# The last unit of a bidirectional state-space mixer gets an order of its own, with the first sequence's spectra and taps inside it

## The chip, the core and the metric

The kernel runs on one core of a Trainium2 chip. A core has TensorE (PE, matrix products; its weight loads are listed as PEld), VectorE (DVE), ScalarE (ACT), GpSimd (POOL) and SyncE (SP, which here issues the DMAs). Each engine works through its own queue in order and waits on semaphores for the others. Matrix products land in PSUM, everything else lies in SBUF; large arrays lie in HBM. The metric is the device time of one execution in microseconds.

## The reference

The input is x, 8 sequences of 1024 tokens with 128 channels, in float32. Layer 0 is a group norm and an attention with 4 heads. Layer 1 has two parts, each added to its input, each behind a layer norm over the channels:

```
t = t + h_f + h_b           # two selective state-space mixers on ln(t), forward and on the reversed sequence:
                            #   project to z, x, B, C, dt; causal convolution of 4 taps; silu;
                            #   chunks of 64: Y = (C B^T * decay) xdt + C state exp(A); state passes on
                            #   y = (Y + D x) * silu(z), scaled by rsqrt(mean y^2), times out_proj
t = t + stu(ln(t))          # spectral filters: out = sum_k  fftconv(phi_k, u) * sigma_k^0.25 * M_k
                            #   (for U+ and U-), plus taps: sum over i < 3 of shift(u, i) * M_u[i]
```

`stu` is taken from one of four banks, which a hard gumbel choice selects.

## The kernel before, in words

`fast_kernel` (L46) has four parts: attention; the mixer; the first spectral stage (forward transforms and taps); and the second (products per frequency, L1412 to L1490, and the transform back, L1514).

**The mixer** runs over 16 units, `Unit(b, d)`: sequence b, direction d = 0 or 1. All five queues follow the order in which the program text issues (`ALL_IN_ORDER`). One pass of the loop at L1194 does unit u, and beside it the tail of the unit before (`last`) and the beginning of the next (`following`). A unit's own steps are:

- `turn_x` (L946): x turned on PE (sx), times dt on DVE (xdt). `weigh_start` (L859): ec on POOL. `turn_b` (L964): B turned and C B^T (sb), copied by ACT (bg). `between` (L854): exp of the decays lm on ACT.
- `decayed_x` (L982): bg masked causally and xdd, on DVE. `project_z`, `activate_z` (L910, L915): pz on PE, silu on ACT (zs).
- `chunk_states` (L992): pst on PE. `pass_states` (L1009): one copy and 28 small DVE steps, each on the one before; after chunks 7 and 14 DMAs copy states to the other half of the partitions (moved).
- `weigh_decays` (L1036): lm times bg on DVE, in two halves. `outputs` (L1044): 64x64 matmuls into sy.
- The tail: `add_x` (L1074) y from sy on DVE; `gate` (L1089) y times zs on DVE, its square on ACT; `end` (L1165): `project_out` (spo), `square_sums` (misc) with a copy by ACT (sums), `turn_sums` (rms_v on DVE, rms on POOL); `scale_rows` (L1133) on ACT; `add_rows` (L1139) into the residual X[b] on DVE, and for d = 1 a store to xd; `reload` (L1145) brings X[b] back in another token order, four neighbouring tokens to a partition.

After the loop, L1285 to L1292 do the last unit's tail alone. PSUM is divided into two pools of two buffers each, `ps_w` and `ps_s`; a buffer is written again when its last reader is done.

**Layer norm** is split: `normalize` (L444) takes the statistics (8 bn_stats and 8 bn_aggr on DVE, `rsqrt` on POOL), `normalized` (L453) a shift on DVE and 8 activations on ACT (ln_x). In the loop, units with d = 1 normalize sequence b + 2 for the mixer; the last unit normalizes sequence 0 in its reloaded form, for the spectral stage.

**The first spectral stage** (L1388) is one loop over b, 0 to 8, with PE, DVE, ACT and POOL in order. `transform(b)` (L1328): 8 transposes of ln_x into cpt; two blocks of 4 products with the cosine and sine table (pf); a copy by ACT (later), two sums on DVE (sd), 6 sums on POOL (sp); a store to ud in HBM; and cpt copied by ACT into ut. `regress(b, k)` (L1369): 12 products of shifted ut with the taps (pu), added to X by DVE. `turned(n)` (L1311) turns a quarter of the mixing matrices (md, mdt, me) and shares cpt's PSUM buffer. One pass does the transform of b, normalizes b + 1, and does the taps of b - 1; then X[b - 1] is stored to xa.

Of the kernel before, what the change touches and what calls it, by code (L numbers as in the profile page):

```python
# [45 lines left out]
def fast_kernel(ctx: ExitStack, tc: tile.TileContext, a: dict, out: bass.AP, bad: bass.AP):  # L46
# [477 lines left out]


# [236 lines left out]
    with ExitStack() as s:  # L762
# [219 lines left out]
        def decayed_x(u):  # L982

            nc.vector.tensor_tensor(u.gm, u.gm, upto[u.d].unsqueeze(1).to_broadcast([P, NT, L]), ALU.mult)
            u.xdd = p1.tile([P, NT, NH, HP], F32, tag="xdd", name=f"xdd{u.tag}")
            for i in range(2):
                js = slice(4 * i, 4 * i + 4)
                nc.vector.tensor_tensor(
                    u.xdd[:, js], u.xdt[:, js], u.rest.rearrange("p h j -> p j h")[:, js].unsqueeze(3).to_broadcast([P, 4, NH, HP]), ALU.mult
                )  # L990
# [18 lines left out]
        def pass_states(u):  # L1009

            u.state = p1.tile([P, 2 * NT - 1, 2, HP], F32, tag="state", name=f"state{u.tag}")
            u.moved = p1.tile([P, NT, 2, HP], F32, tag="moved", name=f"moved{u.tag}")
            for k, (j, c) in enumerate(u.chunks[:-1]):
                if k == 0:
                    nc.vector.tensor_copy(u.state[:, 0], u.pst[c][:, j])
                else:
                    for h in range(2):
                        nc.vector.scalar_tensor_tensor(  # L1018
                            u.state[:, k, h, :],
                            u.state[:, k - 1, h, :],  # L1020
                            u.dec[:, c, h, j : j + 1],
                            u.pst[c][:, j, h, :],
                            ALU.mult,
                            ALU.add,
                        )
                if k in (7, 14):
                    for r in range(2):

                        ks = [m for m in range(0 if k == 7 else 8, k + 1) if u.chunks[m + 1][1] != r]
                        to = slice((1 - r) * L, (2 - r) * L)  # L1030
                        nc.sync.dma_start(
                            u.moved[to, ks[0] // 2 : ks[-1] // 2 + 1],
                            u.state[r * L : (r + 1) * L, ks[0] : ks[-1] + 1 : 2],
                        )
# [39 lines left out]
        def add_x(u):  # L1074

            u.y = p1.tile([P, 2, T], F32, tag="y", name=f"y{u.tag}")
            by_chunk = "p (j c l) -> p c j l"
            for n in range(2):
                for c in range(2):
                    nc.vector.scalar_tensor_tensor(  # L1080
                        u.y[:, n, :].rearrange(by_chunk, j=NT, c=2)[:, c],
                        u.xs[:, n, :].rearrange(by_chunk, j=NT, c=2)[:, c],
                        dcol[u.d][:, n : n + 1],
                        u.py[c][:, n],
                        ALU.mult,
                        ALU.add,
                    )
# [6 lines left out]
        def project_out(u, js):  # L1094
            if js[0] == 0:
                u.po = wide_psum(ps_s, f"spo{u.tag}").rearrange("p (j e) -> p j e", j=NT)
# [68 lines left out]
        def end(u):  # L1165

            project_out(u, range(4))
            misc = wide_psum(ps_s, f"misc{u.tag}")
# [25 lines left out]
        for at, u in enumerate(units):  # L1194
            following = units[at + 1] if at + 1 < len(units) else None
# [4 lines left out]
            if following and u.d == 1:  # L1200
                turn_decays(following)
            if at == 0:
                between(u, AF.Relu, 1.0)
            if following:
                take_decays(following)
# [8 lines left out]
            if following:  # L1214
                project_x(following, 0)
                copy_x(following, 0)
# [3 lines left out]
            if following:  # L1220
                project_x(following, 1)
                copy_x(following, 1)
            if early_decays:
                add_decays(after_it)
            decayed_x(u)
            weigh_decays(u, 0)
            if last:
                end(last)
            if early_decays:
                turn_decays(after_it)  # L1230
            if following:
                first_tap(following, 0)
            if last:
                scale_rows(last)
            b = u.b + 2 if following else 0
            norm = None
            if u.d == 1 and b < B:
# [6 lines left out]
            if following:  # L1244
                convolve(following, 0, range(pad - 1))
# [4 lines left out]
            if following:  # L1250
                first_tap(following, 1)
            if norm:
                mv = norm[0]
                norm = mv, rsqrt(bridge, mv[:, :, 1], NT, 1.0, 1e-5, "ln_r")
                if following:
                    behind(begun[-1], following.convolved, "beside the states")
            if following:
                from_row(following, following.convolved)
# [3 lines left out]
            norming = normalized(b, bridge, *norm) if norm else iter(())  # L1262
# [4 lines left out]
            if following:  # L1267
                convolve(following, 0, range(pad - 1, pad))
                activate_x(following, 0)
                between(following, AF.Relu, 1.0)  # L1270
                project_bc(following)
                activate_bc(following)
                convolve(following, 1)
# [3 lines left out]
            if following:  # L1277
                activate_x(following, 1)
# [5 lines left out]
            last = u  # L1284
        add_x(last)  # L1285
        for n in range(2):
            gate(last, n)
        end(last)
        scale_rows(last)
        add_rows(last)  # L1290
        reload(last)
# [7 lines left out]
    with ExitStack() as s:  # L1299
# [4 lines left out]
        with ExitStack() as s2:  # L1304
# [23 lines left out]
            def transform(b):  # L1328
# [3 lines left out]
                for j in range(NT):  # L1332
                    nc.tensor.transpose(pt[:, j // 4, j % 4, :], un[:, j // 4, j % 4, :], ident)  # L1333
                sp = p2.tile([P, NF // FC, NB, 2, 4, FC], F32, tag="sp", name=f"sp{b}")
                for k in range(NB):
                    pf = ps_f.tile([P, 4, 2, NF], F32, tag="f", name=f"pf{b}_{k}")
                    for r in range(4):
                        nc.tensor.matmul(  # L1338
                            pf[:, r].rearrange("p i f -> p (i f)"),
                            lhsT=un[:, k, r, :],  # L1340
                            rhs=fwd[:, r].rearrange("p i f -> p (i f)"),
                            start=True,
                            stop=True,
                        )

                    sd = p2.tile([P, 2, 2, 2, NF], F32, tag="sd", name=f"sd{b}_{k}")
                    later = p2.tile([P, 2, 2, NF], F32, tag="later", name=f"later{b}_{k}")
                    nc.scalar.copy(  # L1348
                        later.rearrange("p r i f -> p (r i f)"), pf[:, 2:4].rearrange("p r i f -> p (r i f)")
                    )  # L1350
                    for i, op in enumerate((ALU.add, ALU.subtract)):
                        nc.vector.tensor_tensor(sd[:, i], pf[:, 0:2], later, op)  # L1352
                    to = sp[:, :, NB - 1 - k].rearrange("p c i q f -> p q i c f")
                    sd = sd.rearrange("p s r i (c f) -> p s r i c f", f=FC)
                    for q, op in ((0, ALU.add), (2, ALU.subtract)):
                        nc.gpsimd.tensor_tensor(to[:, q], sd[:, 0, 0], sd[:, 0, 1], op)

                    for q, i, op in ((1, 0, ALU.add), (1, 1, ALU.subtract), (3, 0, ALU.subtract), (3, 1, ALU.add)):
                        nc.gpsimd.tensor_tensor(to[:, q, i], sd[:, 1, 0, i], sd[:, 1, 1, 1 - i], op)  # L1359
                nc.sync.dma_start(  # L1360
                    ud[:, :, b].rearrange("c p k i q f -> p c (k i q f)"), sp.rearrange("p c k i q f -> p c (k i q f)")
                )

                ut = uts[b] = p2.tile([P, 4, NB * P + 1], F32, tag="ut", name=f"ut{b}")
                nc.gpsimd.memset(ut[:, :, 0:1], 0.0)
                for k in range(NB):
                    nc.scalar.copy(ut[:, :, 1 + k * P : 1 + (k + 1) * P], pt[:, k])

            def regress(b, k):  # L1369

                xq = X[b].rearrange("p (k r) c -> p k r c", k=NB)
                po = ps_o.tile([P, 4, C], F32, tag="o", name=f"pu{b}_{k}")
                for r in range(4):
                    for i in range(KU):
                        at = 1 + k * P - (i > r)
                        nc.tensor.matmul(  # L1376
                            po[:, r, :],
                            lhsT=uts[b][:, (r - i) % 4, at : at + P],
                            rhs=m_u[:, i, :],
                            start=(i == 0),  # L1380
                            stop=(i == KU - 1),
                        )
                nc.vector.scalar_tensor_tensor(xq[:, k], po, keep[:, k : k + 1], xq[:, k], ALU.mult, ALU.add)
# [3 lines left out]
            norms[1] = normalize(p2, 1)  # L1387
            for b in range(B + 1):  # L1388
# [7 lines left out]
                if b:  # L1396
                    regress(b - 1, 0)
                    if b <= 4:
                        turned(b - 1)
                    regress(b - 1, 1)  # L1400
                    nc.sync.dma_start(xa[b - 1].rearrange("p k r c -> p (k r) c"), X[b - 1])
# [957 lines left out]
```

## Time and profile before

| | |
|---|---|
| time, median of 3 runs | 1477.29 us (1474.59 to 1480.68) |
| the profiled execution, its time | 1471.66 us |
| its span | 1469.9 us |
| mean granted clock of PE | 0.978 |
| PE busy | 1340.2 us (91%) |
| PEld busy | 841.3 us (57%) |
| DVE busy | 1095.4 us (75%) |
| ACT busy | 912.9 us (62%) |
| POOL busy | 505.9 us (34%) |
| HBM read, written | 78.15 MB, 34.08 MB |

Busy time is the time in which an engine has an instruction in work; matmuls are pipelined and their ends are modelled, so a busy PE is not one at its peak. The granted clock is the share of full speed that the throttle gave PE. In rows of the timeline the columns are start, length, engine, line, operation, output and inputs, count; in rows of waits: total, times, longest. Line numbers are those of the kernel before.

In the trace the last unit's own work begins with sx at 1009.49 us, its row scaling ends at 1058.2, and the first spectral stage's first transposes (cpt) begin at 1058.27. The first product of the second spectral stage (pg) begins at 1151.23.

### The profile page before, as it was taken

What the parts mean: (1) busy time and instruction counts of PE and PEld (TensorE: products, weight loads), DVE (VectorE), ACT (ScalarE), POOL (GpSimd) and SP (SyncE); (2) the same over time, 40 slices, a digit from 0 to 9 for tenths busy, and PEclk for the clock granted to TensorE, in tenths of its full rate; (3) what the DMA queues carried; (4) which work ended last, traced back from release to release, by engine and by line L of the source; (5) the groups of instructions that cost most, each with busy time, mean ns of one, the idle gap of its engine ahead of it and who ended that gap; (6) DMA issues with size and microseconds to landing.
All of it is one profiled execution on the core that took longest, in us unless ns stands there. A gap on an engine that the chain in (4) does not pass through costs nothing. (4 is left out here: it accounts for less than half of the span.)

```text
span 1469.9 us, 45286 instructions
## 1 busy us (share of the span) xinstructions
PE 1340.2 (91%) x19782; PEld 841.3 (57%) x19782; DVE 1095.4 (75%) x2138; ACT 912.9 (62%) x1421; POOL 505.9 (34%) x510
## 2 busy tenths in 40 slices
PE   5999999999998889998989899998599899999977
PEld 2323333333333556665656566655489899999963
DVE  6788888788767687878787877787555577777755
ACT  3766666766765777777777777666355455555520
POOL 3336966866201332323232323233186211111100
PEclk9999999999999999999999999999799999999989
DMA  7101111110002334444444444341258422322258
GB/s 182 35 1 30 44 36 37 51 50 9 8 1 58 74 73 98 92 91 96 90 95 90 92 91 97 88 90 29 69 191 218 128 76 68 91 71 76 68 144 322
DMA packets 139382, 123.09 MB, mean 84 GB/s; under 512 B 44808, under 2 KB 118152, under 8 KB 135080
## 3 DMA queue, kind: packets, MB, share of 16 engines
q1 hardware_dynamic: 137064, 115.93, 30.8%
q10 hardware_dynamic: 2112, 4.19, 0.7%
q8 instruction: 157, 2.57, 0.7%
q14 instruction: 49, 0.40, 0.1%
HBM read 78.15 MB, written 34.08 MB: 76 GB/s over the span
## 5 line engine op out<-in xcount | busy, mean ns | idle before, releaser
L633 ACT ACTIVATE pr<-pt 128x1024 f32<-128x1024 f32 x256 | 247.9, 1021 | 114.3 <-PE pt L628 112.7
L658 DVE TENSOR_TENSOR two<-pr,pr 128x1024 f32<-128x1024 f32 x128 | 162.8, 1312 | 20.7 <-ACT pr L633 19.8
L1433 ACT COPY gs<-pg 128x512 f32<-128x512 f32 x256 | 132.5, 602 | 63.4 <-PE pg L1420 47.5
L1431 DVE COPY gs<-pg 128x512 f32<-128x512 f32 x256 | 158.8, 684 | 14.1 <-PE pg L1420 8.9
L628 PE MATMUL pt<-q,k 32*128 32x512 f32 x1024 | 159.3, 653 | 7.0 <-ACT pr L633 4.7
L1420 PE MATMUL pg<-taps,mst 32*128 32x128 f32 x4096 | 145.2, 280 | 4.4 <-ACT gs L1433 3.5
L1420 PEld LDWEIGHTS pg<-taps,mst 32*128 32x128 f32 x4096 | 133.3, 188 | 16.4 <-issue 11.4
L649 PE MATMUL po<-pr,v 128*32 128x512 f32 x1024 | 139.3, 602 | 0.0
L925 PE MATMUL pb<-bxt,wbc 128*128 128x512 f32 x256 | 115.6, 604 | 14.7 <-ACT zs L916 14.7
L1454 PE MATMUL py<-gs,u 128*32 128x128 f32 (+1 forms) x4096 | 127.8, 277 | 0.2 <-DVE gs L1431 0.2
L861 POOL TENSOR_TENSOR ec<-ec,ct 128x2048 f32<-128x2048 f32 x16 | 72.6, 4536 | 153.1 <-ACT ct L941 141.0
L903 DVE SCALAR_TENSOR_TENSOR xs<-xp,cw,xs 128x1024 f32<-128x1024 f32 x96 | 121.8, 1282 | 4.6 <-issue 1.7
L1454 PEld LDWEIGHTS py<-gs,u 128*32 128x32 f32 (+1 forms) x4096 | 112.0, 140 | 7.5 <-DVE gs L1431 0.4
L1443 POOL TENSOR_SCALAR u<-u 128x512 f32<-128x512 f32 x16 | 24.0, 1497 | 227.2 <-DMA u<-ud 120.1
L628 PEld LDWEIGHTS pt<-q,k 32*128 32x128 f32 x1024 | 47.6, 186 | 85.5 <-issue 32.3
L1129 POOL TENSOR_TENSOR rms<-rms_v,mhalf 128x8 f32<-128x8 f32 x16 | 27.9, 1742 | 187.5 <-DVE rms_v L1127 187.5
L925 PEld LDWEIGHTS pb<-bxt,wbc 128*128 128x128 f32 x256 | 47.7, 191 | 73.1 <-issue 59.1
L1018 DVE SCALAR_TENSOR_TENSOR state<-state,dec,pst 128x64 f32<-128x64 f32 x448 | 87.3, 275 | 1.1
L848 POOL TENSOR_TENSOR lm<-cs,lm 128x2048 f32<-128x2048 f32 x16 | 57.9, 3621 | 60.6 <-DVE sp_u L508 30.8
L649 PEld LDWEIGHTS po<-pr,v 128*32 128x32 f32 x1024 | 27.7, 109 | 88.2 <-issue 84.1
L1099 PE MATMUL spo<-wo,y 128*128 128x128 f32 x512 | 71.0, 288 | 7.9 <-DVE y L1091 7.8
L957 DVE TENSOR_TENSOR xdt<-sx,dt 128x1024 f32<-128x1024 f32 x32 | 37.9, 1220 | 52.9 <-PE sx L954 52.9
(278 smaller groups left out, 2797.9 us busy)
## 6 DMA issues: line engine op xcount, KB each, us to landing
lm<-cd SPq DMA_DIRECT2D x32, 512.0 KB
ec<-cd SPq DMA_DIRECT2D x32, 512.0 KB
ud<-sp SPq DMA_DIRECT2D x8, 1024.0 KB
u<-ud SPq DMA_DIRECT2D x32, 256.0 KB
yd<-sums SPq DMA_DIRECT2D x32, 256.0 KB
moved<-state SPq DMA_DIRECT2D x48, 128.0 KB
yt<-yd SPq DMA_DIRECT2D x6, 1024.0 KB
X<-in_x SPq DMA_DIRECT2D x8, 512.0 KB
```

The costliest lines, as they stand in the source:

```text
L628: nc.tensor.matmul(pt[:, i, :], lhsT=k[rows, j * P : (j + 1) * P], rhs=q[rows, cols], start=True, stop=True)
L633: nc.scalar.activation(pr[:, 2 * g : 2 * g + 2, :].rearrange("p i t -> p (i t)"), pt.rearrange("p i t -> p (i t)"), AF.Exp, scale=SCALE,)
L649: nc.tensor.matmul(po[rows, :], lhsT=vs[b][:, j, rows], rhs=pr[:, h, :], start=(j == 0), stop=(j == NT - 1))
L658: nc.vector.tensor_tensor(two, sums["pr"][:, 2 * g : 2 * g + 2, :], pr[:, 2 * g : 2 * g + 2, :], ALU.add)
L861: t = nc.gpsimd.tensor_tensor(u.ec, u.ec, u.ct.unsqueeze(1).to_broadcast([P, NH, NT, L]), ALU.mult)
L903: u.convolved = nc.vector.scalar_tensor_tensor(acc, xp[:, at : at + T], cw[u.d][:, n, i : i + 1], acc, ALU.mult, ALU.add)
L925: nc.tensor.matmul(u.pb[:, i * 512 : (i + 1) * 512], lhsT=wbc[u.d][:, k, :], rhs=xt[:, at : at + 512], start=(k == 0), stop=(k == KC - 1),)
L1018: nc.vector.scalar_tensor_tensor(u.state[:, k, h, :], u.state[:, k - 1, h, :], u.dec[:, c, h, j : j + 1], u.pst[c][:, j, h, :], ALU.mult, ...
L1420: nc.tensor.matmul(pts[g][:, e, :], lhsT=mst[rows, n * 4 + e, :], rhs=taps[rows, cols].rearrange("p f q m i -> p (f q m i)"), start=True, ...
L1431: nc.vector.tensor_copy(to, frm)
L1433: nc.scalar.copy(to, frm)
L1454: nc.tensor.matmul(py[t * 32 : t * 32 + 32 - 16 * m, q // 2, :], lhsT=u[:, i, m:, :, :, q * FC + f].rearrange("p k b i -> p (k b i)"), rhs ...
```

## The change

The loop over units ends before the last one, and the last unit is written out by hand. In it, `decayed_x` comes before the masking (now `causal`), z is projected before the states, `pass_states` takes the chunks it shall do and is called twice, and `end` is given its PSUM pool. The bodies of `transform` and `regress` become functions of their own (same operations), and for sequence 0 they are called inside the last unit, with tiles that reuse buffers of the mixer (ut0, sp0, sd0). Sequence 0 is normalized in unit (6, 1); sequence 1's statistics are taken in unit (7, 0) and its activations are made in the last unit. The loop of the first spectral stage begins at b = 1. The operations of the whole kernel are the same in kind, shape and number.

```diff
-            b = u.b + 2 if following else 0
+            b = (u.b + 2) % B
             norm = None
-            if u.d == 1 and b < B:
+            if u.d == 1 or u.b == B - 1:
                 norm = normalize(bridge, b, later=True)
...
-            norming = normalized(b, bridge, *norm) if norm else iter(())
+            norming = normalized(b, bridge, *norm) if u.d else iter(())
...
+        u = units[-1]
+        un = xns.pop(0).rearrange("p (k r) c -> p k r c", k=NB)
+        turn_x(u)
+        weigh_start(u, u.convolved)
+        turn_b(u)
+        between(u, AF.Exp, -1.0)
+        decayed_x(u)
         add_x(last)
+        causal(u)
         for n in range(2):
-            gate(last, n)
-        end(last)
+            project_z(u, n)
+            activate_z(u, n)
+        chunk_states(u)
+        pt = wide_psum(ps_w, "cpt0").rearrange("p (k r c) -> p k r c", k=NB, r=4)
+        turn_spectra(un, pt)
+        gate(last, 0)
+        gate(last, 1)
...
+        copy_turned(ut, pt)
+        pass_states(u, range(8))
+        end(last, ps_w)
+        pass_states(u, range(8, 2 * NT - 1))
         scale_rows(last)
...
+        making = spectra(0, "lm")
+        next(making)
+        weigh_decays(u, 0)
+        weigh_decays(u, 1)
         add_rows(last)
-        reload(last)
+        for _ in making:
+            pass
+        reload(stored)
+        outputs(u, 0)
+        outputs(u, 1)
+        making = spectra(1, "ec")
+        next(making)
+        add_x(u, "xdd")
+        gate(u, 0)
+        gate(u, 1)
+        po = wide_psum(ps_w, "pu0").rearrange("p (k r c) -> p k r c", k=NB, r=4)
+        for k in range(NB):
+            regress(0, k, ut, po[:, k])
+        norming = normalized(1, bridge, *norm)
+        next(norming)
+        for _ in making:
+            pass
+        store_spectra(0, sp)
+        end(u, ps_s)
+        for _ in norming:
+            pass
+        for k in range(NB):
+            add_taps(0, k, po[:, k])
+        store_residual(0)
+        scale_rows(u)
+        add_rows(u)
+        reload(u)
...
-            norms[1] = normalize(p2, 1)
-            for b in range(B + 1):
+            norms[2] = normalize(p2, 2)
+            for b in range(1, B + 1):
                 if b + 2 < B:
                     norms[b + 2] = normalize(p2, b + 2)
...
-                if b:
-                    regress(b - 1, 0)
-                    if b <= 4:
-                        turned(b - 1)
-                    regress(b - 1, 1)
-                    nc.sync.dma_start(xa[b - 1].rearrange("p k r c -> p (k r) c"), X[b - 1])
+                if b > 1:
+                    taps_of(b - 1, 0)
+                if b <= 4:
+                    turned(b - 1)
+                if b > 1:
+                    taps_of(b - 1, 1)
+                    store_residual(b - 1)
```

The block's spectra are a generator: its first step issues the four products and ACT's copy, its second the sums on DVE and POOL.

```python
    def block_spectra(k, un, pf, sd, later, sp):
        for r in range(4):
            nc.tensor.matmul(
                pf[:, r].rearrange("p i f -> p (i f)"),
                lhsT=un[:, k, r, :],
                rhs=fwd[:, r].rearrange("p i f -> p (i f)"),
                start=True,
                stop=True,
            )
        nc.scalar.copy(later.rearrange("p r i f -> p (r i f)"), pf[:, 2:4].rearrange("p r i f -> p (r i f)"))
        yield
        for i, op in enumerate((ALU.add, ALU.subtract)):
            nc.vector.tensor_tensor(sd[:, i], pf[:, 0:2], later, op)
...
```

## The prediction

> **What bounds the kernel now.** I read the page's 40 slices first (where TensorE is not full, and at what clock), then the chain that ended last, then the waits and the timeline of the stretch that the change touches, 1008 to 1092 us.
>
> The slices, one line per engine, about 37 us a digit:
>
> ```profile
> PE   5999999999998889998989899998599899999977
> ...
> PEclk9999999999999999999999999999799999999989
> ```
>
> TensorE is full nearly everywhere; one slice inside, the 29th (1029 to 1066), falls to 5, with the clock at 7. The hole is the mixer's last unit and what follows it. By stretches of that hole (length, busy time of PE, PEld, DVE, ACT, POOL, then granted clock):
>
> ```profile
> 1020.60:1027.80 7.20, 7.20 (x43) 4.04 (x42) 4.54 (x20) 2.53 (x9) 3.34 (x3) 0.92 0.00 0
> 1027.80:1035.50 7.70, 2.03 (x65) 1.77 (x64) 5.58 (x29) 3.24 (x4) 1.01 (x1) 0.77 0.15 30
> 1035.50:1042.50 7.00, 5.74 (x248) 5.49 (x248) 1.38 (x4) 3.19 (x8) 0.00 (x0) 0.76 0.42 118
> 1042.50:1046.50 4.00, 0.00 (x0) 0.03 (x1) 4.00 (x6) 0.11 (x1) 0.00 (x0) 0.90 0.00 0
> 1046.50:1058.30 11.80, 8.15 (x51) 6.24 (x51) 1.22 (x3) 4.55 (x11) 1.64 (x1) 0.75 0.01 2
> 1058.30:1067.40 9.10, 6.22 (x25) 4.95 (x25) 8.85 (x42) 2.71 (x6) 4.98 (x6) 0.81 0.73 222
> 1067.40:1081.60 14.20, 13.76 (x80) 11.43 (x80) 4.96 (x20) 8.85 (x20) 12.80 (x27) 0.88 0.26 80
> ```
>
> No engine is full here: one engine at a time works, and the next waits for it. The waits of 1008 to 1092 name the hand-overs (total us, times, longest):
>
> ```profile
> PE spo L1099 <- DVE y L1091: 7.8, 4, 4.0
> ...
> PE sy L1066 <- DVE state L1018: 5.7, 1, 5.7
> DVE y L1080 <- PE sy L1066: 5.6, 1, 5.6
> ...
> PE cpt L1333 <- ACT y L1137: 3.4, 1, 3.4
> ...
> PE sy L1066 <- DMA moved<-state: 1.2, 1, 1.2
> ```
>
> So the last unit is a latency chain (states, outputs, gate, output projection, row scale), and cpt0, the first transposes of the spectra, waits for its end at 1058.27. In the chain of waits, cpt0 to cpt2 reads:
>
> ```profile
> 1058.27 1.09 PE cpt L1333 x8
> ...
> 1066.44 0.36 DVE b_shift L455
> 1066.84 2.81 ACT ln_x L460 x7
> 1069.69 0.86 PE cpt L1333 x2
> ...
> 1077.51 3.19 ACT ln_x L460 x8
> 1080.70 0.90 ACT me L1319
> 1081.65 1.09 PE cpt L1333 x8
> ```
>
> From cpt2 on a sequence takes 11.2 to 9.7 us, all TensorE. Of the next stages nothing changes.
>
> **The change, part by part.** All times are against the profiled execution, span 1469.9 and time 1471.66.
>
> *Two normalizations move forward.* Sequence 0's goes into unit (6,1), sequence 1's statistics into (7,0). Each adds 8 bn_stats and 8 bn_aggr (1.64 + 0.62 on DVE) and two GpSimd instructions (0.20 + 1.64); (6,1) also 8 activations (3.2). Unit (5,1) has all of these and took 34.61 us from ec to ec; (6,1), without, 34.67. So: nothing. In (7,0) DVE stood 3.07 us for pst before the states, which covers 2.26; uncovered it would cost 2.3. GpSimd's lm there ends 1.84 later, at 998.2, and its reader (ACT, 1003.71) does not notice.
>
> *The last unit's order.* I walk the compiled order from sx (1009.49), which nothing moves. DVE: xdt 1010.5 to 1012.9, xdd 2.35, add_x 2.71, causal 0.69, gates of (7,0) 2.35, done 1020.6. TensorE: sb to 1013.87, pz 3.6, pst 1.96, done 1019.5 (before: 1029.84). ACT is the tight one: bg copy, table load 1.28, exp 2.0, table load 1.28, silu 1.94, squares 2.15, ut copies 1.08, to 1024.7. DVE's first half of the states ends 1023.65. Now a new wait: rms_v of (7,0) stands in DVE's queue between the two halves. It needs misc, which needs the ut copies (its PSUM buffer held cpt0): misc to 1025.8, sums 0.37, turned sums, 1027.2. Behind it in DVE's queue are 14 state steps, both lm multiplications, X, sd0; DVE stands 3.5 us. The states then end 1027.4 + 2.73 = 1030.15, against 1035.67: 5.5 gained.
>
> *From states to outputs.* lm multiplied: 1031.3 and 1032.5. pf0_0 (1.74) fits in before that; scaling of (7,0)'s rows (GpSimd 1.64, ACT 2.18) is beside. The outputs stop half-way for the last moved state. Before, this resumed 5.05 after the last state (1035.67 to 1040.72); in (6,1) 6.73 after; packets ended about 2.5 after. I take 5.05, the same unit's: 1035.2; bounds 2.5 to 6.73. The rest of the outputs took 1.74: done 1036.95 (before 1042.46).
>
> *What is added on the path.* TensorE then does pf0_1 (half of a 3.46 pair, 1.73) and pu0 (48 records, 5.36) before spo: 1044.05. Beside it DVE does add_x 2.73 and the gates 2.35, to 1042.0. So 7.1 us of moved work costs 2.05; without that cover it would cost all 7.1. On ACT squares and half of ln_x1 end at 1044.7, before sums asks for it. On SP the store of the spectra is queued before xa, xd and the md loads; it waits for GpSimd at about 1046.6, the others are not ready earlier.
>
> *From spo to cpt1.* [...] In the last unit the chain from the first spo to the end of rms_v was 7.8 us (1046.51 to 1054.29); in the unit before, at full granted clock, 4.9:
>
> ```profile
> 984.06 2.31 PE L1099 MATMUL spo<-wo,y 128*128 128x128 f32 x16
> 986.30 1.07 PE L1111 MATMUL misc<-zs,ones 128*32 128x256 f32 x16
> ```
>
> [...] Now 7.1 us of matmuls stand right before spo[...]. I take 4.9, since the unit before shows it behind busy TensorE: rms_v at 1049.0. Then rms on GpSimd 1.64, scaling 2.18: 1052.95. cpt1 starts at 1053.0, where cpt0 stood at 1058.27.
>
> *GpSimd.* Twelve sp instructions (3.1 us per half) now precede rms on its queue; the second half runs 1043.4 to 1046.5. [...] rms took 2.48 instead of 1.64 beside the lm multiplication (989.1). At that ratio 3.1 becomes 4.7, end 1048.1, still before 1049.0: nothing. Rms itself at 2.48 would cost 0.84, twice; that is in the range.
>
> *The spectra stage.* Before, cpt0 to cpt2 took 23.38. Now it begins with cpt1; DVE still has to do two sequences' statistics first, so b_shift comes 8.1 to 8.2 after the start as before, ln_x2 8.57 after, 3.19 long, then me0 and cpt2: 12.8. The transforms of sequence 0 and pu0 are gone; the limit is DVE and ACT, no longer TensorE. Could the statistics be hidden, cpt2 would come 3 us earlier; they are queued behind X, which waits for the scaling, so no. From cpt2 on all is as before.
>
> Sum: cpt2 at 1053.0 + 12.8 = 1065.8 instead of 1081.65: 15.85 less, 5.3 of it in the last unit, 10.6 in the spectra stage. On the profiled run 1455.8. The runs' median is 1477.29, 5.6 above the profile, so the same saving gives 1461.4.
>
> **The rivals.** *The last unit is not shortened* (new waits on misc and the ACT row eat the 5.3): only the spectra stage saves 10.6, so 1466.7. For it: ACT has no gap from 1013.9 to 1024.7, and DVE stands for it. Against: the unit had 20 us without TensorE.
>
> *The filler lies wholly on the path*: cpt0 1.0, both pf 3.5 and pu0 5.4 delay the unit by 9.9, 0.7 remains, 1476.6. Against: most of it stands where TensorE was idle.
>
> *Slower*: the granted clock. The busier hole could leave the stage after it at less than full clock; it has about 76 us of TensorE-bound sequences from cpt2. At 0.78 (less than any later stretch shows, near the 0.75 to 0.77 in the hole) they take 76 x (1/0.78 - 1) = 21.4 more: +5.6, 1482.8. It decides from a clock of 0.83 down. Against: 1.00 in 1092.9 to 1150.4 under the same load.
>
> **How the numbers follow.** The main case 0.76, time 1461.4. Its terms: moved state -2.5 to +1.7, rms 0 to +1.7, so 1459 to 1465, and the runs' own spread of 3 either way: 1456 to 1468. Last unit not shortened 0.15 (1466.7), filler on the path 0.06 (1476.6), slower 0.03. Range 1454 to 1469: it takes in the first rival and two us below for waits that fall out better. A measurement here can tell about 0.5%, 7.4 us. Faster by more: main case and first rival, 0.91; within: 0.06; slower: 0.03.
>
> **What would show it.** Right: pst done near 1019.5; DVE idle about 3.5 before rms_v; last state near 1030; outputs waiting for moved near 1035; spo near 1044 in 2.0 to 2.3 per 16; cpt1 near 1053, cpt2 12.8 later; every later stage as long as before. Wrong: spo starting past 1047, rms waiting for sp on GpSimd, cpt2 waiting for md or a PSUM buffer, sequences from cpt2 longer than 11.2.

## The result, and the profile after

The changed kernel takes 1465.67 us (median of 7 runs, 1462.86 to 1471.08) where the kernel before takes 1477.29 (7 runs, 1474.12 to 1480.68): ratio 0.9922, 95% interval [0.9901, 0.9943], so about 11.5 us less. The forecast of 1461.4 had 15.9 less. The profiled execution took 1462.86 us, with a span of 1461.1.

The slices of the changed kernel (one line per engine, 36.5 us a digit):

```profile
PE   5999999999998888999898898999789899999977
...
PEclk9999999999999999999999999999889999999989
```

The hole in the 29th slice went from 5 to 7, and its clock from 7 to 8. It became shallower and did not close. What is left of it, by stretches (length, then busy time of PE, PEld, DVE, ACT and POOL, granted clock, DMA share, GB/s):

```profile
1034.80:1037.75 2.95, 0.00 (x0) 0.00 (x0) 0.95 (x2) 0.00 (x0) 2.52 (x5) 0.85 0.17 65
1037.75:1040.80 3.05, 3.05 (x105) 2.93 (x104) 0.00 (x0) 0.00 (x0) 0.53 (x2) 0.50 0.02 5
1040.80:1044.20 3.40, 3.40 (x11) 2.81 (x11) 3.37 (x5) 0.00 (x0) 0.00 (x0) 0.58 0.02 5
1044.20:1049.40 5.20, 5.20 (x49) 5.20 (x48) 2.89 (x5) 4.16 (x7) 2.82 (x6) 1.00 0.00 0
...
1070.60:1077.00 6.40, 6.39 (x26) 5.70 (x27) 0.95 (x2) 0.58 (x1) 3.23 (x7) 0.70 0.69 211
```

Read the first column of TensorE together with the clock. In the first row TensorE does nothing for 2.95 us: the outputs stand half-way. In the second it works without a gap, on the rest of the outputs, and needs 3.05 us for what took 1.74 before, because the clock is at 0.50. The row of before:

```profile
1040.72:1042.46 1.74, 1.74 (x104) 1.61 (x104) 0.00 (x0) 0.00 (x0) 0.00 (x0) 1.00 0.07 20
```

In the third, pf0_1 takes 3.4 us (1.73 forecast), at 0.58. Only pu0, in the fourth, has the full clock. The last row is the third sequence's cpt2 and pf2 at 0.70.

A clock in between is a mean of two. In the traces of the kernel before and of the changed one the granted clock is either 1.00 or 0.50, and each stretch at 0.50 that the end does not cut off lasts 3.41, 6.83 or 10.24 us. Here one begins 2.08 us after TensorE has stopped and covers the rest of the outputs and nearly all of pf0_1:

```profile
1034.78:1036.86 2.08, 0.00 (x0) 0.00 (x0) 0.97 (x2) 0.00 (x0) 1.63 (x3) 1.00 0.26 97
1036.86:1043.69 6.83, 5.94 (x111) 5.28 (x111) 2.86 (x5) 0.00 (x0) 1.42 (x4) 0.50 0.02 5
```

The waits of 1008 to 1092 say what came before each slow row (total us, times, longest):

```profile
DVE y L1145 <- PE sy L1131: 5.1, 1, 5.1
PE sy L1131 <- issue: 4.0, 2, 3.0
PE cpt L528 <- ACT me L1435: 4.0, 1, 4.0
PE cpt L528 <- ACT y L1200: 3.4, 1, 3.4
```

There are three waits of TensorE of 3.0, 3.4 and 4.0 us. The 5.7 us for DVE's states and the 7.8 for the gates, which led TensorE's waits before, are gone.

"issue" means that the trace has no event for the end of that wait. The forecast took it for the moved state, and so do the expectations of the experiments below. The semaphore events of the trace say otherwise: the last moved state is in at 1033.88, 2.74 us after DVE computed it, the product that waits for it starts at 1034.56, and only at 1034.78 does TensorE stop. What comes shortly before the end of the stop (1037.75) is a packet of 16 KB on a queue of the kind "instruction", at 1035.37 to 1036.35. The page's lines of the whole execution, and the line of that queue for 1035.30 to 1036.40 alone (packets, MB, share):

```profile
PE 1336.9 (91%) x19782; PEld 838.2 (57%) x19782; DVE 1094.3 (75%) x2138; ACT 912.1 (62%) x1421; POOL 504.1 (34%) x510
q8 instruction: 157, 2.57, 0.8%
q8 instruction: 1, 0.02, 5.5%
```

TensorE has 39,811 records in the trace (products, weight loads and 247 others, 242 of them on semaphores), or 254 to each of the 157 packets; VectorE, ScalarE and GpSimd together have a tenth of that. TensorE has nine stops of 0.7 us or more in this trace, between 540 and 1040 us, that no event ends. From one of them to the next it is 768 to 2048 records, each time a multiple of 256, whether the product that comes next reads the states, the moved states or lm; and each ends 1.2 to 1.5 us after a packet of this queue. My reading is that the outputs stand for TensorE's next instructions; no event shows it. The reload's 512 KB are moved at 1033.38 to 1035.47, and the packet starts as they end. The last unit of the kernel before is another case: there the moved state was in only at 1040.68, and the product started at 1040.72.

The chain from the scaling of rows to the third sequence:

```profile
1066.48 3.18 ACT ln_x L460 x8
1069.66 0.90 ACT me L1435
...
1070.61 1.97 PE cpt L528 x8
1072.58 4.43 PE pf L539 x16
```

ACT's part is as forecast, 3.18 and 0.90. The transposes behind it take 1.97 us, where the next sequence's take 1.09.

spo of the last unit, to be held against the row of unit (7, 0) that the forecast relied on (2.31 us there; start, length, line, shapes):

```profile
1049.36 1.95 PE L1162 MATMUL spo<-wo,y 128*128 128x128 f32 x16
```

The whole hole shifts from execution to execution with the 1000 us ahead of it: the unit's transposes of x (sx, the piece behind the wait for ACT's xs, 1009.49 us before) start at 1010.74 here, and at 1007.9 to 1017.8 in the runs below. So I measure from there: to the first transpose of the next stage (the unit), and from that to the first product of the filter matrices (pg; the stage). Each value is from one profiled execution; ratios are of timed runs to the kernel before. Only the intervals of experiments 7, 9 and 12 lie clear of the changed kernel's; what a single step is worth is read from the traces.

| kernel | unit | stage | sum | ratio [95%] |
|---|---|---|---|---|
| before | 48.78 | 92.96 | 141.74 | 1 |
| changed | 47.17 | 83.80 | 130.97 | 0.9922 [0.9901, 0.9943] |
| 1 spectra between the outputs | 43.15 | 84.31 | 127.46 | 0.9902 [0.9882, 0.9922] |
| 2 spare products in the wait | 44.81 | 85.66 | 130.47 | 0.9923 [0.9895, 0.9952] |
| 3 spare products in the stage | 45.77 | 81.96 | 127.73 | 0.9892 [0.9862, 0.9922] |
| 4 reload behind the outputs | 45.73 | 84.88 | 130.61 | one run, 1464.56 us |
| 5 order alone | 42.28 | 92.50 | 134.78 | 0.9956 [0.9937, 0.9975] |
| 6 = 1 and a quarter of the taps | 43.87 | 84.92 | 128.79 | 0.9882 [0.9857, 0.9908] |
| 7 = 1 and third statistics | 44.26 | 80.30 | 124.56 | 0.9859 [0.9833, 0.9884] |
| 8 = 1 and 3 | 42.80 | 82.09 | 124.89 | 0.9884 [0.9853, 0.9916] |
| 9 = 6, 7 and spare behind spo | 42.62 | 81.85 | 124.47 | 0.9866 [0.9837, 0.9895] |
| 10 moved states on ACT's queue | 42.78 | 84.35 | 127.13 | one run, 1459.45 us |
| 11 reload behind the store | 42.84 | 84.35 | 127.19 | 0.9907 [0.9890, 0.9924] |
| 12 = 10 and third statistics | 43.95 | 79.37 | 123.32 | 0.9882 [0.9865, 0.9898] |

The change took 1.6 us out of the unit (5.3 forecast) and 9.2 out of the stage (10.6 forecast).

### The profile page after: what moved, and what is told of

It reads as the page before. It is cut to its first block, busy times and chain, and to the rows that moved or that the text cites. A ratio compares the mean times of both kernels' runs of the same rounds, so it can differ in the third digit from the quotient of the medians.

```text
span 1461.1 us, 45273 instructions
## 1 busy us (share of the span) xinstructions
PE 1336.9 (91%) x19782; PEld 838.2 (57%) x19782; DVE 1094.3 (75%) x2138; ACT 912.1 (62%) x1421; POOL 504.1 (34%) x510
## 5 line engine op out<-in xcount | busy, mean ns | idle before, releaser
L728 PE MATMUL pd<-two,ones 128*32 128x512 f32 x512 | 74.4, 612 | 0.2
```

Source lines behind the costliest of these rows:

```text
L728: nc.tensor.matmul(sums["d"][(2 * g + i) * DH : (2 * g + i + 1) * DH, :], lhsT=ones[:, :DH], rhs=two[:, i, :], start=(j == 1), stop=(j == ...
```

## The experiments

My first theory: the mechanism of the forecast holds, and what is missing is the halved clock (0.50), which TensorE gets after standing 3.0 us in the outputs (for the moved state, as I then thought), and the 0.70 after 4.0 us for ACT's me. The rivals: the reload of X6, which SyncE issues right behind the moved states, holds up their landing; or the moved-in work itself, by its place in the queues.

**1, the second half of the spectra between the two halves of the outputs.**

```diff
         outputs(u, 0)
-        outputs(u, 1)
         making = spectra(1, "ec")
         next(making)
+        outputs(u, 1)
         add_x(u, "xdd")
```

> The changed kernel with one step moved: the second block's spectra (pf0_1, four products and ACT's copy) go between the two halves of the last unit's outputs, into the wait for the moved state. Nothing is added or left out. Clock theory (the rest of the outputs and pf0_1 were slow, 3.06 and 3.44 us, because TensorE had stood idle and its granted clock had fallen to 0.50 to 0.58): the outputs' rest takes 1.7 again, pf0_1 costs nothing on the path, the outputs end at about the same landing + 1.7, pu0 follows at once; spo starts about 4.7 us earlier, and the run is about 4.5 us faster than the changed kernel, a ratio to before of about 0.989. Rival (the time lies in the late landing of the moved state and in the order of the queue, and the clock is beside the point): only pf0_1's place is won, at most 3.4, and the outputs' rest still takes about 3.0.

Measured: 1461.37 us, ratio 0.9902 [0.9882, 0.9922]. The windows of this kernel, from the wait on:

```profile
1034.81:1036.21 1.40, 0.39 (x17) 0.29 (x18) 0.00 (x0) 0.58 (x1) 1.40 (x4) 1.00 0.00 0
1036.21:1038.07 1.86, 1.86 (x113) 1.79 (x112) 0.00 (x0) 0.00 (x0) 0.54 (x2) 1.00 0.05 9
1038.07:1043.79 5.72, 5.65 (x48) 5.46 (x49) 5.70 (x9) 1.73 (x2) 0.00 (x0) 1.00 0.01 3
```

pf0_1 now fills 2.0 us of the wait. 1.0 is left, the clock stays at 1.00, and the rest of the outputs takes 1.86 us instead of 3.05. The outputs still go on 6.6 us after the last state. They stop 8 products earlier than in the changed kernel (136 records instead of 144), and the 8 products and 8 weight loads of pf0_1 now stand ahead: counted in TensorE's instructions the stop is at the same place, and it is not at the same product. The unit is 4.0 us shorter.

**2, three spare products (128x512, result unused) in the same wait.** Nothing else is moved; the kernel does more work.

```diff
         outputs(u, 0)
+        spare = wide_psum(ps_w, "spare")
+        for i in range(3):
+            nc.tensor.matmul(spare[:, :512], lhsT=ident, rhs=fwd[:, 0:2]..., start=True, stop=True)
         outputs(u, 1)
```

> The changed kernel plus three spare products of 128x512 (about 2.7 us) between the two halves of the last unit's outputs; nobody reads them, nothing else is moved. They do no work of the kernel, only keep TensorE from standing idle while it waits for the moved state. Clock theory: outputs' rest 1.7 instead of 3.06, pf0_1 1.73 instead of 3.44, so spo starts about 3 us earlier although 2.7 us of work are added. Rival (not the clock): no stretch becomes shorter, and the unit is 0 to 2.7 us longer.

Measured: behind the spare products the outputs take 2.75 us for 128 records, 0.34 of it a stop, at clock 1.00; pf0_1 takes 1.99, and the unit is 2.4 us shorter although TensorE has 2.8 us more to do. The added work takes nothing off the path, so this is the clock. The gain is not seen in the timed ratio (0.9923 [0.9895, 0.9952]): in this execution the stage behind gave 1.9 back, where cpt2 and pf2 ran slower still (7.4 us from the start of one to the end of the other).

**3, four spare products in the stage**, behind the transposes of the first filter spectra, where TensorE waits 4.0 us for ACT's me.

```diff
                 if b <= 4:
                     turned(b - 1)
+                if b == 1:
+                    spare = ps_o.tile([P, 4, C], F32, tag="o", name="spare")
+                    for i in range(4):
+                        nc.tensor.matmul(spare..., lhsT=ident, rhs=fwd[:, 0:2]..., start=True, stop=True)
```

> The changed kernel plus four spare products of 128x512 (about 3.6 us) behind the first turned matrices (mdt0) in the spectral stage, where TensorE stands 4 us for ACT before cpt2; nobody reads them. Clock theory: cpt2 and the two pf after it take 1.09 and 3.47 instead of 1.97 and 4.43, and cpt2 to cpt3 goes back to 11.2 from 12.76, about 1.5 us faster in all. Rival (the first full sequence is longer because of DMA or PSUM buffers that the change has brought together): cpt2 to cpt3 stays near 12.8.

Measured, the windows of the spare products and of cpt2 with pf2:

```profile
1066.09:1069.95 3.86, 3.60 (x10) 1.33 (x8) 1.79 (x15) 3.81 (x9) 3.86 (x9) 1.00 0.54 181
1069.95:1074.60 4.65, 4.65 (x27) 4.24 (x28) 1.05 (x2) 0.59 (x2) 3.35 (x7) 1.00 0.51 157
```

cpt2 and pf2 take 4.65 us instead of 6.4, and from cpt2 to cpt3 it is 10.92 instead of 12.76. The ratio is 0.9892 [0.9862, 0.9922]. The unit was left alone here and shows how far it varies: the rest of the outputs is slow again (3.05), but pf0_1 takes 1.99 us and not 3.44, and the unit 45.8 instead of 47.2. The stretch at 0.50 lasts 3.41 us here (1038.04 to 1041.45) and in experiment 4, and 6.83 in the changed kernel's trace: it differs from one execution to the next. So of a unit's difference to 47.2, up to 1.4 us can be this; against 45.75, the mean of experiments 3 and 4, experiment 1 gains 2.6 us and experiment 2 still 0.9.

**4, the reload behind the outputs.**

```diff
-        reload(stored)
         outputs(u, 0)
...
+        reload(stored)
         store_spectra(0, sp)
```

> The changed kernel with the reload of X6 (512 KB) moved behind the last unit's outputs on SP's queue; nothing else. It asks what the 6.6 us from the last state to the outputs' resumption are. If the reload's data delays the moved state's landing: 2 to 3 us less, outputs resume 4 us after the last state. If the landing has its own latency, as in unit (7,0) of the kernel before, which had no reload behind it and still took 6.4: no change, 5.0 to 6.7.

Measured: wait 2.97 us, state to product 6.6, rest of the outputs 3.05: nothing changed. I first took that as the end of the rival. It was not: no instruction between the two places is SyncE's, so SyncE issued the reload right behind the moved states as before. The experiment moved a line of the program and nothing on the queue. The eleventh does it properly.

**5, the order alone.** The new unit without the spectra and taps; sequence 0's spectra and taps, and sequence 1's normalization, stay in the stage.

```diff
-        pt = wide_psum(ps_w, "cpt0")...
-        turn_spectra(un, pt)
...
-        making = spectra(0, "lm")
-        next(making)
...
-        for k in range(NB):
-            regress(0, k, ut, po[:, k])
...
-            for b in range(1, B + 1):
+            for b in range(B + 1):
```

> The last unit in its new order, with the first sequence's spectra and taps left where they were (after the mixer, as in the kernel before) and the second sequence normalized there too. Clock theory: the moved state is waited for as in the changed kernel (about 6.6 us after the last state), the rest of the outputs runs on the halved clock (3.05 us), the gates end where they did, 35.1 us after the unit's first product, but spo now starts cold, after some 5 us without a product, and takes 7.8 us to rms_v instead of 4.6: the next stage's first transposition 46.5 to 47.5 us after the unit's first product, where the kernel before has 48.8 and the changed one 47.2. So order alone is worth 1.3 to 2.3 us, and without the 10.7 of the spectra the time is 1472 to 1476, a ratio of 0.998 to 1.000. Rival (the moved-in work, by its order on TensorE and ScalarE, costs what the unit did not gain): without it the unit ends at 43.5 as forecast, 5.3 us saved, ratio 0.9964.

Measured: 0.9956 [0.9937, 0.9975], and a unit of 42.28 us. My expectation of 46.5 to 47.5 was wrong, and the rival's number was near: the moved-in work does cost the changed unit 4.9 us. The windows show how (first half of the outputs, wait, second half, then spo to rms_v):

```profile
1032.50:1037.30 4.80, 4.80 (x160) 4.61 (x160) 2.17 (x2) 0.01 (x1) 0.00 (x0) 0.50 0.61 150
1037.30:1037.85 0.55, 0.00 (x1) 0.00 (x1) 0.00 (x0) 0.00 (x0) 0.00 (x0) 0.50 0.00 0
1037.85:1039.42 1.57, 1.57 (x88) 1.43 (x88) 0.00 (x0) 0.00 (x0) 0.00 (x0) 0.94 0.05 10
...
1043.46:1050.60 7.14, 6.86 (x46) 5.61 (x47) 1.08 (x2) 2.38 (x3) 0.00 (x0) 0.66 0.01 2
```

Without pf0_0 ahead of them the outputs begin on the slow clock, and that is free: they fill the time until TensorE goes on from the stop (6.58 us after the last state, 6.61 in the changed kernel), 0.55 us remain, and the second half is fast (1.57 us at clock 0.94). The stop comes at record 160 of the outputs instead of 144, with 32 instructions of cpt0 and pf0_0 gone ahead of it. In the changed kernel, with pf0_0 ahead, the first half has the full clock (2.44 us) and reaches the stop earlier, waits 2.97, and the slow clock falls on the second half and pf0_1, where it counts. Between the two kernels: states 1.5 us (cpt0 and the taps' copies ahead of misc, as forecast), second half 1.5, from there to spo 4.5, and from spo on 2.65 won back by the full clock.

**6, a quarter of the taps as well in the wait** (on top of 1).

```diff
         next(making)
+        po = wide_psum(ps_w, "pu0")...
+        regress(0, 0, ut, po[:, 0], range(1))
         outputs(u, 1)
```

> The second block of spectra between the two halves of the outputs as in the first experiment, and behind it the first quarter of the taps (0.65 us of products) as well, into the 1.0 us of wait that was left there. Clock theory: the outputs' rest still starts when the state has landed, the taps behind it are 0.65 us shorter and end at or before the gates, so spo starts with the gates, 0.7 us earlier than in the first experiment and 4.7 earlier than in the changed kernel: ratio 0.9895. Rival: the gates' end already sets spo (the taps end beside it), then nothing: ratio 0.9902 as there.

Measured: from the end of the stop to spo 7.15 us instead of 7.58, so 0.43 of 0.65; spo then starts 0.16 us behind the gates' end, which leaves no more to win. Nothing shows in time: 0.9882 [0.9857, 0.9908] and 0.9902 overlap. This execution came into the unit on the slow clock (sx 2.70 us instead of 1.86), so its 43.87 says nothing against 43.15.

**7, the third sequence's statistics in the unit** (on top of 1), in DVE's idle 3.8 us before rms_v; its activations issued ahead of cpt1.

```diff
+        norms[2] = normalize(resid, 2, later=True)[0]
         end(u, ps_s)
...
+        norms[2] = norms[2], rsqrt(resid, norms[2][:, :, 1], NT, 1.0, 1e-5, "ln_r")
         scale_rows(u)
...
-            norms[2] = normalize(p2, 2)
+            for _ in normalized(2, p2, *norms.pop(2), wide=p2):
+                pass
```

> The first experiment, and the third sequence's statistics taken in the unit, in VectorE's idle 3.8 us ahead of rms_v, its scaling and shifting put ahead of the second sequence's transpositions. If VectorE's statistics and ScalarE's eight activations behind them set the distance from the second sequence's transpositions to the third's (12.70 us in every run), ScalarE does the activations in its idle 4.6 us instead, me of the first quarter ends at about 10 us after the second sequence's transpositions, and the distance falls from 12.7 to 10.0 to 10.5: 2.3 to 2.7 us on top of the first experiment's 4.0, ratio 0.988 to 0.989. Should the products after it also be on the full clock, 1.8 more. Rival: the load of the filter spectra or the taps' copies bind there; then the distance stays at 12 or more, ratio 0.990.

Measured: 1456.98 us, 0.9859 [0.9833, 0.9884]. From cpt1 to cpt2 10.28 us instead of 12.70, from cpt2 to cpt3 10.91 instead of 12.76: the wait ahead of cpt2 is now 1.1 us, and cpt2 runs on the full clock.

**8, experiments 1 and 3 together.** (Both edits above.)

> The first and the third experiment together: the second block of spectra between the halves of the outputs, and four spare products (3.6 us, their result unused) behind the transposition of the filter spectra. Clock theory: the two savings lie in different stages and add, 4.0 and 1.8 us: 5.8 below the changed kernel, ratio to the kernel before 0.988 to 0.989. Rival (the clock is a budget, and warm time here is paid for by a lower clock later): 4.0 or less, ratio 0.990, and a lower granted clock in the stages behind.

Measured: unit 42.80, stage 82.09; in the trace the two add, as the clock theory had it. 1457.06 us, 0.9884 [0.9853, 0.9916], an interval that holds the rival's 0.990 too. From cpt2 to pg the clock is at 1.00 throughout (1063.3 to 1132.75), so time at the full clock here is not paid for there.

**9, experiments 6 and 7, and three spare products behind spo**, where TensorE waits 3.4 us for the scaled rows.

```diff
         end(u, ps_s)
+        spare = wide_psum(ps_w, "spare")
+        for i in range(3):
+            nc.tensor.matmul(spare[:, :512], lhsT=ident, rhs=fwd[:, 0:2]..., start=True, stop=True)
```

> The experiment with the third sequence's statistics, the first quarter of the taps in the rest of the wait as well (0.4 us measured), and three spare products (2.7 us, result unused) behind the last unit's spo, in the 3.4 us in which TensorE waits for the scaled rows. Clock theory: the second sequence's transpositions and products, 1.17 and 5.27 us on the halved clock there, take 1.1 and 3.6 us; ScalarE, which copies their result, goes on as much earlier, so the distance from these transpositions to the next falls from 10.3 to 9 or less where the load of the filter spectra does not bind: 1.3 to 2.1 us below the run without, ratio 0.9845 to 0.985. Rival (the load of the filter spectra ends at a time of its own, and holds the third sequence): the products are fast and the wait behind them is longer by the same, ratio 0.9857 as before.

Measured: pf1 takes 3.62 us at clock 1.00 (5.27 in the seventh), and nothing comes of it: 0.9866 [0.9837, 0.9895]. The waits of TensorE behind spo:

```profile
PE mdt L1441 <- DMA md<-md: 3.2, 1, 3.2
PE cpt L528 <- ACT me L1443: 1.1, 1, 1.1
PE cpt L528 <- ACT y L1200: 0.8, 1, 0.8
```

The rival's case: the filter spectra's load arrives when it arrives, and the time won ahead of it is waited (3.2 us; 1.9 in the seventh), after which cpt2 is slow again (1.97 us, granted clock 0.51).

**10, the moved states on ACT's queue.** The second pair of the last unit only.

```diff
-        pass_states(u, range(8, 2 * NT - 1))
+        pass_states(u, range(8, 2 * NT - 1), nc.scalar)
```

> The changed kernel, with the second pair of moved states of the last unit issued from ScalarE's queue instead of SyncE's. Theory: the 6.6 us from the last state to the first product that reads a moved one is a transfer's own latency, then it stays at 6 to 7 us and nothing else moves by more than 0.5. Rival: it is SyncE's queue (two transfers one after the other, the reload behind them); then the wait falls towards the 5.05 us that the forecast took, 1.5 us less, and the unit with it. In both cases ScalarE scales the rows of the unit before up to 2 us later, which has no one waiting in this stretch.

Measured: from the last state (1031.21) to the product (1036.17) 4.96 us instead of 6.6. My theory, a fixed latency, fell. The wait is 1.33, the clock stays at 1.00, the rest of the outputs takes 1.74 and pf0_1 1.99, and the unit is 42.78: 1.6 us of waiting less make the unit 4.4 shorter (3.0 against experiments 3 and 4). On SyncE's queue the reload, no longer behind the moved states, ran before them (issued at 1026.41). But the moved states come no earlier: they are in 2.83 us after the last state, 2.74 in the changed kernel. What comes earlier is the instruction packet, at 1033.83 to 1034.75, 0.1 us behind their packets.

**11, the reload behind the store of the spectra**, which waits for GpSimd.

```diff
-        reload(stored)
         outputs(u, 0)
...
         store_spectra(0, sp)
+        reload(stored)
         end(u, ps_s)
```

> The changed kernel, with the last residual's reload issued behind the store of the first sequence's spectra. (In the experiment before it that put the reload behind the outputs, SyncE still issued it 0.6 us behind the moved states, since nothing in between is SyncE's: it told nothing.) Now SyncE first waits for GpSimd's last spectra, some 18 us after the moved states. Theory: the 512 KB behind the moved states hold their landing up; then the first product that reads one starts 4.9 to 5.1 us after the last state, as it did when they went by ScalarE's queue, instead of 6.6; the wait is 1.3 us instead of 3.0, the rest of the outputs 1.75 us instead of 3.06, and the second sequence's first transposition 42.8 to 43.5 us after the unit's first transposition but one, instead of 47.2: ratio 0.989. Rival: it is SyncE's queue itself; then 6.6 us, 45.8 to 47.2, ratio 0.992.

Measured: 1460.3 us, 0.9907 [0.9890, 0.9924]. SyncE's issues in the changed kernel (start, length):

```profile
1030.79 1.25 SPq L1096 DMA_DIRECT2D moved<-state  x2
1032.09 0.61 SPq L1210 DMA_DIRECT2D X<-xd  x1
```

and in this one:

```profile
1031.25 1.25 SPq L1096 DMA_DIRECT2D moved<-state  x2
1047.24 0.38 SPq L560 DMA_DIRECT2D ud<-sp  x1
1047.67 1.30 SPq L1210 DMA_DIRECT2D X<-xd  x1
```

with these windows (wait, rest of the outputs, pf0_1):

```profile
1035.23:1036.62 1.39, 0.00 (x1) 0.00 (x1) 0.98 (x2) 0.00 (x0) 0.93 (x2) 1.00 0.00 0
1036.62:1038.36 1.74, 1.74 (x105) 1.67 (x104) 0.00 (x0) 0.00 (x0) 1.74 (x5) 1.00 0.05 9
1038.36:1040.29 1.93, 1.93 (x11) 1.73 (x11) 1.91 (x3) 0.00 (x0) 0.40 (x1) 1.00 0.00 0
```

The moved states leave on the same queue, and without the 512 KB behind them the product starts 5.01 us after the last state (1031.61). So it is the reload, not the queue. What comes later with it is again not the moved state, which is in 2.73 us after the last state (2.74 with the reload), but the instruction packet, here at 1034.26 to 1035.18 (queue line for 1034.20 to 1035.20):

```profile
q8 instruction: 1, 0.02, 5.8%
```

In the ten traces of the new order with the reload behind the moved states (the changed kernel, experiments 1 to 9) this packet starts within 0.1 us of the end of the reload's packets. In experiments 10, 11 and 12 it starts 0.1 to 0.3 us behind the moved states' own.

**12, experiments 10 and 7 together**, the order of the unit as changed.

> The moved states by ScalarE's queue as in the tenth kernel, the order of the unit otherwise as changed, and the third sequence's statistics taken in the unit as in the seventh. If the two add, the unit is 4.4 us shorter than the changed kernel's (42.8 instead of 47.2) and the distance from the second sequence's transpositions to the third's 10.3 instead of 12.7, with 1.8 more from the full clock behind it: 8 to 8.6 us below the changed kernel, ratio 0.986. Rival: the statistics need VectorE's idle time in the unit, of which the faster unit has less, or the filter spectra's load binds; then 6 us, ratio 0.988.

Measured: 1456.22 us, 0.9882 [0.9865, 0.9898], the rival's number in time. In the trace the parts do add: state to product 5.06 us, cpt1 to cpt2 10.10, cpt2 to cpt3 10.91, and the sum of 123.32 is 7.7 below the changed kernel, with a unit that began on the slow clock (sx 2.92 us instead of 1.86). Versions 7, 8, 9 and 12 are 1.2 to 1.4% below the kernel before, and their intervals do not tell them apart.

## Why the prediction was right, and 4 us too hopeful

Point by point, from sx to pg, where 15.85 us less were forecast and the profiled execution has 10.77:

- *The early normalizations cost nothing*: right. From the first sx of unit (7, 0) to the last unit's it took 33.55 us with the statistics and 33.56 without.
- *The last unit's order*: right. DVE stood 3.36 us for rms_v (3.5 forecast), and the last state came 20.40 us after sx (20.66).
- *"The outputs stop half-way for the last moved state"* and *"I take 5.05"*: wrong in its cause, and the first term that was mis-sized. The outputs went on 6.61 us after the last state, +1.56, but not for a moved state, which was in after 2.74, before they stopped. What came ahead of the stop's end was an instruction packet (1035.37 to 1036.35), behind the reload. That a stop came at all where the forecast had one is luck. The two rows that it weighed are of different kinds: the last unit's 5.05 did end with the moved state, 16 of whose 448 packets ran only at 1039.13 to 1039.97, behind an instruction packet of 1038.22 to 1039.14; the 6.73 of unit (6, 1) did not, as its states were in after 2.85 us and no event ends its stop. Unit (7, 0) stopped until 6.37 us with no reload behind it.
- *"The rest of the outputs took 1.74"*: the step that failed. That row stood behind a wait of 1.18 us; now the wait is 2.97, and behind it the clock is 0.50: 3.05, +1.31.
- *pf0_1 and pu0 before spo*: 8.56 us instead of 7.1, +1.46, all of it pf0_1: 3.44 us on the slow clock, 1.99 at 1.00 in experiments 10 and 11.
- *From spo on*: right. 4.57 us to the end of rms_v (4.9 in the row of unit (7, 0), 7.8 in the last unit's own), and GpSimd's spectra took 3.07 us. That does not test the 4.7 that was weighed, from rms beside VectorE's lm (2.48 instead of 1.64), since VectorE stood idle for all but the first 0.5 us of it. The forecast asked for TensorE's clock at this one place, and not behind the waits that its own sums produced.
- *cpt1 to cpt2*: right, 12.70 (12.8).
- *"From cpt2 on all is as before"*: wrong by 1.52. What left the stage had kept TensorE busy; now it stands 3.98 us ahead of cpt2 and comes back at clock 0.70. Experiment 3 shows it.

Together the four terms are 5.85 us; the last state, spo to cpt1 and cpt1 to cpt2 came 0.76 earlier than forecast, which leaves the 5.1 between 15.85 and 10.77. The clock's part is in the rows: 0.50 to 0.52 behind waits of 2.97 to 3.02 us, in the changed kernel and in experiments 3 and 4, where the step down comes 2.1 to 2.5 us after TensorE has stopped, and 1.00 behind 1.0 to 1.4 us in experiments 1, 10, 11 and 12. The length of a wait alone does not decide it in the traces: elsewhere in the mixer 0.50 stood behind 2.37 us in the kernel before (900.07 to 902.44), and 1.00 behind 3.06 us in the changed kernel (482.62 to 485.68):

```profile
902.44:905.74 3.30, 3.30 (x88) 3.18 (x88) 0.00 (x0) 3.26 (x7) 2.64 (x1) 0.50 0.03 5
485.68:489.09 3.41, 3.41 (x8) 1.62 (x9) 3.41 (x4) 1.88 (x2) 0.00 (x0) 1.00 1.00 233
```

Nor does it set how long the clock stays down: pf0_1 took 3.44 us in one execution and 1.99 in two others of the same order, behind waits of 2.97 to 3.02.

The rivals: "the last unit is not shortened" (1466.7) came nearest in time, and not by its mechanism: its waits on misc and ACT did not cost what it needs, as the last state came 0.26 us earlier than forecast. The granted clock, named for the stage behind, did its work inside the hole instead. *"Could the statistics be hidden, cpt2 would come 3 us earlier ... so no"* was too quick: taken in the unit, they bring 2.4 to 2.6 and the clock of cpt2.

What is not settled: what TensorE stands for in a stop that no event ends, and what sets the time of the instruction packet; no event of the traces shows either. That the reload delays the packet is read from the times of the two and from experiments 10 to 12.

## What to carry to other kernels

Moving work into a hole of a latency chain changed the clock of what follows: work out every wait of TensorE that the new order leaves. In the hole of the changed kernel the rows behind the waits of 2.97, 3.38 and 3.98 us have a granted clock of 0.50, 0.76 and 0.70, with stretches at 0.50 of 3.41 or 6.83 us. Put independent products into such a wait and not behind it (experiment 1: the same work, 2.6 to 4.0 us less in the unit). Look also at what is left behind where the work was taken away: the stage that lost its filler paid part of the gain back (1.52 us from cpt2 on). And before naming what a stop waits for, look for the event that ends it. Where there is none, count the engine's instructions and look for packets of the kind "instruction": with a bulk load of 512 KB just ahead of such a packet the outputs went on 1.6 us later, and the unit, with the clock behind the longer wait at 0.50, took 2.9 to 4.3 us more.

## What was not expected of the hardware

- TensorE stops at places that follow the count of its instructions. Its nine longer stops in the mixer that no event ends (0.74 to 2.97 us) are 768 to 2048 records apart, each time a multiple of 256, and end 1.2 to 1.5 us after a 16 KB instruction packet. With 512 KB on the DMA engines just before, the stop in the outputs ended 6.6 us after the last state, without them 5.0, while the moved states were in after 2.7 us in both.
- Slow clock was free once: in experiment 5 the first half of the outputs at clock 0.50 (4.80 us instead of 2.44) ended just ahead of the stop's end, which it had to wait for anyway, and the unit was the shortest of all.
- Spare products shortened a unit: 2.8 us of useless work in the wait made it 0.9 to 2.4 us shorter.
